# First scans of a hybrid layer: stores of u, delta, gate, B and C on ScalarE's queue, and the product delta times u three turns later

## The chip, the core and the metric

The kernel runs on one core of a Trainium2 chip. Its engines are TensorE (PE, with its weight loads as PEld), VectorE (DVE), ScalarE (ACT), GpSimd (POOL) and SyncE (SP). SP, ScalarE and GpSimd also issue DMAs, each in the order of its own program. The metric is the time of one launch on the device, in microseconds; the median of several launches is given. The profile is of one execution.

## What is computed

Two layers over `x` of shape (4, 64, 64, 128): four images of 4096 tokens with 128 channels. The first layer is a group norm and a state-space block with three scan directions, whose result is added to `x`. The second is an attention layer and a layer of experts. The change lies in the first layer:

```python
xz = einsum('pd,bld->bpl', in_proj_w, x)            # 2 x 256 rows
x, z = split(xz)
x = silu(causal_conv1d(x, conv_w, conv_b))          # u
x_dbl = einsum('rd,bdl->brl', x_proj_w, x)          # 8 rows for delta, 16 for B, 16 for C
delta = softplus(dt_w @ dt_raw + dt_b)
# over l, for each of 256 rows d and 16 states n:
h = h * exp(delta * A) + (delta * u) * B
y = sum_n h * C
out = (y + D * u) * silu(z)                         # z: the gate
```

This is done for three orders of the tokens (forward, backward, sliced), and the three results are added.

## The kernel before

All numbers are float32. A scan of one image and one order is cut into 4 chunks of 1024 tokens. Two kinds of work make it up.

**The inputs** (class `Inputs`). For each image the generator `norm` reads `x`, transposes it, and writes the group norm's result into `xn`. For each of 3 orders and 4 chunks the generator `of_chunk` then does the following. TensorE multiplies `xn` with the input projection, into which the convolution's taps have been folded (L412). ScalarE's Silu writes `u`, two blocks of 128 rows by 1024 tokens (L419). TensorE makes the rows for delta, B and C from `u` (L426), and ScalarE copies them to `xd` (L428). TensorE makes delta's argument (L438), and ScalarE's Softplus writes delta into the tile `r` (L445). For the chunks that `early` names (all twelve of image 0 and the first two of image 1), VectorE multiplies `r` and `u` in place into `u`, as delta times u (L453); for the other chunks that is done later, beside the attention. Everything is stored to DRAM: `keep` (L396) stores `u`, delta and the product in 1 MB each, L439 and L440 store B and C in 64 KB each. The generator `gate` makes silu(z) for a chunk of 1024 tokens and stores it (L379), also 1 MB. All of these stores are issued by SP.

Tiles come from pools: the tag `u` has two buffers, shared by `u` and the gate's `s_g`; `xd` and `r` have one each. A writer of a tile waits until the earlier user of its buffer, a store included, is done.

**The scans** (class `Scans`, generator `of_image`). One step takes 16 rows d by 8 states n, which fill the 128 partitions, over 1024 tokens; image 0 has 384 steps. For each pair of steps `load` brings delta (L527, issued by SP) and delta times u (`du`, L527, issued by ScalarE when the scans of image 0 run alone), each repeated over 8 partitions and so 512 KB; for each four steps a piece of `u` (`us`, L532, SP); and for each chunk B and C (L508, SP). Delta has three buffers, `du` four. ScalarE makes exp(delta * A) (L542). VectorE multiplies du and B into `dB` (L551) and runs the scan into `h` (L561). GpSimd keeps the scan's last column (L563) and multiplies by C (L568). TensorE sums over the states (L599). Every four steps VectorE adds D * u (L615), and SP stores the result `o` (L626, L633 or L637 by the order of the tokens).

**The order.** The program's order on each engine is written out by hand: generators yield, and a loop takes turns between them. Each `yield` of a piece of the inputs is one turn. In the stretch concerned the loop is

```python
first = Pace(decays(nc, dirs, ws, inputs), scans.of_image(0, inputs.made, True))
others = Pace(flow(inputs.pieces(range(nb)), 2, 10))
while not first.done:
    others.run(1.4)
    first.run(1.0)
```

so that 1.4 turns of the inputs of all four images are recorded for each turn of the scans of image 0; a scan step has two turns. `flow` keeps two pieces going and takes a turn of each. The first piece's `decays` loads A in 96 small DMAs on SP (L231). A scan step `s` records the loads of step `s + 4`, the exponential of step `s + 3`, and then its own scan and the dB of step `s + 1`. The scans of images 1 to 3 come later, beside image 0's opening and the attention.

Of the kernel before, what the change touches and what calls it, by code (L numbers as in the profile page):

```python
# [16 lines left out]
P = 128  # L17
# [4 lines left out]
NS = 16  # L22
# [4 lines left out]
T = 1024  # L27
# [3 lines left out]
B_ROW, C_ROW, X_ROWS = 8, 40, 104  # L31
# [180 lines left out]
def orders(b):  # L212

    return ORDERS[min(b, 1)]


def early(b, order, c):

    return b == 0 or (b == 1 and order == orders(b)[0] and c < 2)
# [15 lines left out]
class Inputs:  # L235
# [126 lines left out]
    def gate(self, b, g):  # L362
        nc, xn = self.nc, self.normed[b]
        s_g = self.piece.tile([P, 2, T], F32, tag="u", bufs=2, name=f"z_{b}_{g}")
        banks = yield from self.banks(4, f"z_{b}_{g}")
        for m in range(2):
            for i in range(2):
                at = 3 + g * T + i * 512
                nc.tensor.matmul(
                    banks[2 * m + i], self.w_z[:, m * P : (m + 1) * P], xn[:, at : at + 512], start=True, stop=True,  # L370
                )
            yield
        for m in range(2):
            for i in range(2):
                nc.scalar.activation(s_g[:, m, i * 512 : (i + 1) * 512], banks[2 * m + i], AF.Silu)
                self.leave()
        yield
        yield
        nc.sync.dma_start(out=self.sz[b].rearrange("(m p) t -> p m t", p=P)[:, :, g * T : (g + 1) * T], in_=s_g)  # L379
        self.gated[b] += 1  # L380
        yield

    def of_chunk(self, b, order, c):
        while b not in self.normed or (order == 2 and b not in self.sliced):
            yield WAIT
        src = self.sliced[b] if order == 2 else self.normed[b]
        nc, w, key = self.nc, self.ws[order], f"{b}_{order}_{c}"
        made = {
            "delta": self.dram.tile([DI, T], F32, name=f"d_delta_{key}"),
            "du": self.dram.tile([DI, T], F32, name=f"d_du_{key}"),  # L390
            "u": self.dram.tile([DI, T], F32, name=f"d_u_{key}"),
            "bc": self.dram.tile([2, NS, T], F32, name=f"d_bc_{key}"),
        }

        def keep(name, t):
            nc.sync.dma_start(out=made[name].rearrange("(m p) t -> p m t", p=P), in_=t)  # L396

        def reads(k, g):

            at = c * T + g * 512  # L400
            if order == 1:
                end = L + 6 - at - k
                return src[:, end - 512 : end][:, ::-1]
            return src[:, at + k : at + k + 512]

        halves = [slice(g * 512, (g + 1) * 512) for g in range(T // 512)]
        u = self.piece.tile([P, 2, T], F32, tag="u", bufs=2, name=f"u_{key}")
        banks = yield from self.banks(4, f"cv_{key}")
        for m in range(2):
            for g in range(2):  # L410
                for k in range(4):
                    nc.tensor.matmul(  # L412
                        banks[2 * m + g], w["conv"][:, k, m * P : (m + 1) * P], reads(k, g), start=(k == 0), stop=(k == 3)
                    )
                yield
        yield
        for m in range(2):
            for g, cut in enumerate(halves):
                nc.scalar.activation(u[:, m, cut], banks[2 * m + g], AF.Silu, bias=w["conv_b"][:, m : m + 1])  # L419
                self.leave()  # L420
        yield
        xd = self.piece.tile([X_ROWS, T], F32, tag="xd", name=f"xds_{key}")
        for g, cut in enumerate(halves):
            ps = yield from self.bank(f"xd_{key}_{g}")
            for m in range(2):
                nc.tensor.matmul(ps[:X_ROWS], w["x"][:, m, :], u[:, m, cut], start=(m == 0), stop=(m == 1))  # L426
            yield
            nc.scalar.copy(xd[:, cut], ps[:X_ROWS])  # L428
            self.leave()
        keep("u", u)  # L430
        yield
        r = self.piece.tile([P, 2, T], F32, tag="r", name=f"r_{key}")
        banks = yield from self.banks(4, f"dt_{key}")
        for m in range(2):
            for g, cut in enumerate(halves):
                at = 32 * (2 * m + g)
                rows = slice(at, at + R)
                nc.tensor.matmul(banks[2 * m + g], w["dt"][rows, m, :], xd[rows, cut], start=True, stop=True)  # L438
        nc.sync.dma_start(out=made["bc"][0], in_=xd[B_ROW : B_ROW + NS])  # L439
        nc.sync.dma_start(out=made["bc"][1], in_=xd[C_ROW : C_ROW + NS])  # L440
        yield
        yield
        for m in range(2):
            for g, cut in enumerate(halves):
                nc.scalar.activation(  # L445
                    r[:, m, cut], banks[2 * m + g], AF.Softplus, bias=w["dt_proj_b"][:, m : m + 1]
                )
                self.leave()
        yield
        by_early = early(b, order, c)  # L450
        if by_early:
            for m in range(2):
                nc.vector.tensor_mul(u[:, m, :], r[:, m, :], u[:, m, :])  # L453
                yield
        yield
        keep("delta", r)
        if by_early:
            yield
            keep("du", u)
        self.made[b, order, c] = made  # L460
        yield

# [251 lines left out]
class Attention:  # L714

    def __init__(self, tc, ctx, w, gate, cols, ident, bank, dram, t1, w_out, scans, sz, x):
        nc = self.nc = tc.nc
        gate_w, gate_b = gate  # L720
# [799 lines left out]


def tile_kernel(tc, ctx, x, in_proj_w, dirs, out_proj_w, attn, gate, weight1, weight2, out):


# [13 lines left out]
    with ExitStack() as fill:  # L1538
# [10 lines left out]
        with tc.manual_schedule():  # L1549
# [5 lines left out]
            others.rest()  # L1555
    bank = scans.bank = Bank(ctx.enter_context(tc.tile_pool(name="bank", bufs=1, space=PSUM)), 1)
    block = Attention(tc, ctx, attn, gate, cols, ident, bank, dram, t1, w_out, scans, inputs.sz, x)

    following = Pace(*(scans.of_image(b, inputs.made) for b in range(1, nb)))
# [112 lines left out]
```

## Time and profile before

| | |
|---|---|
| Median of 3 runs | 11419.19 us (11400.92 to 11422.68) |
| The profiled execution | 11412.32 us |
| Its span, first to last instruction | 11410.5 us |
| First dB of image 0's scans starts | 97.97 us |
| Last scan of image 0 starts, and takes | 1800.00 us, 2.35 us |
| Moved by DMA between 60 and 1830 us | 403.68 MB |
| of this on SP's queue (q1), on ScalarE's (q10) | 301.45 MB, 101.11 MB |

The page of a profile gives for each engine the time in which it was busy, and for each group of instructions the idle time ahead of it with the instruction that ended it. An arrow such as "u L453 <- ACT r L445" reads: the instruction that writes `u` in line 453 found its engine idle until ScalarE's instruction of line 445, which writes `r`, was done. "SPq" and "ACTq" are the parts of SP and ScalarE that issue DMAs. The first 1812 us of the span are the stretch in which the scans of image 0 run beside all inputs; after it the opening of image 0 and the attention follow.

The largest DMAs that the inputs and scans of this stretch issue, counted between 60 and 1830 us:

| DMA | by | count | KB each |
|---|---|---|---|
| delta into SBUF, for the scans | SP | 192 | 512 |
| du into SBUF, for the scans | ACT | 192 | 512 |
| u to DRAM | SP | 48 | 1024 |
| delta to DRAM | SP | 48 | 1024 |
| gate to DRAM | SP | 16 | 1024 |
| product to DRAM | SP | 14 | 1024 |
| B and C to DRAM | SP | 96 | 64 |

### The profile page before, as it was taken

How to read it: one execution, taken by the hardware profiler on the slowest of the kernel's cores; microseconds unless marked ns; L12 is line 12 of the kernel's file. 1: busy time of each engine (PE TensorE's matmuls, PEld its weight loads, DVE VectorE, ACT ScalarE, POOL GpSimd, SP SyncE). 2: the span in 40 equal slices, each digit the busy share in tenths (PEclk: the TensorE clock that was granted, in tenths of full speed). 3: DMA queues.
4: the chain of work that ended last, by engine and by line, in shares of the span. 5: the costliest groups of instructions: out<-in, count | busy, mean ns of one | idle time of the engine just before them, and what ended most of it. 6: DMA issues, size and time to landing. Idle time of an engine off the chain costs nothing.

```text
span 11410.5 us, 183033 instructions
## 1 busy us (share of the span) xinstructions
PE 9874.3 (87%) x68358; PEld 3273.6 (29%) x68358; DVE 8258.3 (72%) x8405; ACT 9993.7 (88%) x10828; POOL 3790.3 (33%) x3891
## 2 busy tenths in 40 slices
PE   6687792788998889899998899999998999999995
PEld 2233331222222222222222222222222223333323
DVE  6889997888888987999988979988998321111212
ACT  4566672899999999999999999999999999989992
POOL 4777784332323223424333124243331110000000
PEclk8798895899999999999999999999999999999997
DMA  6778897656565665665656755656556332222225
GB/s 188 226 231 230 226 249 198 161 145 156 142 155 155 178 174 146 158 154 142 151 147 160 194 157 156 156 141 151 146 147 162 116 100 72 76 71 84 75 65 186
DMA packets 900980, 1747.52 MB, mean 153 GB/s; under 512 B 203150, under 2 KB 443846, under 8 KB 899830
## 3 DMA queue, kind: packets, MB, share of 16 engines
q1 hardware_dynamic: 764734, 1469.68, 47.9%
q0 software_dynamic: 93856, 156.41, 4.8%
q10 hardware_dynamic: 41496, 109.71, 3.6%
q8 instruction: 537, 8.80, 0.3%
q14 instruction: 357, 2.92, 0.1%
HBM read 1379.76 MB, written 355.47 MB: 152 GB/s over the span
## 4 chain that ended last, share of the span: by engine, by line
PE 38%; ACT 24%; issue 14%; DVE 11%; DMA 10%; POOL 1%; SPq 1%; ACTq 0%; DVEq 0%; POOLq 0%
PE acc L1012 21%; ACT e L1003 20%; PE s L998 10%; DVE h L561 5%; DMA delta<-d_delta 4%; PE cv L412 2%; DMA du<-d_du 2%; DVE dB L551 1%; ACT dA L542 1%; PE y L599 1%; ACT delta L542 1%; PE fo L1169 1%; PE xd L426 1%; PE h L1156 1%; DMA w<-in_L_ffn_weight_dram 1%
## 5 line engine op out<-in xcount | busy, mean ns | idle before, releaser
L1003 ACT ACTIVATE e<-s 128x1024 f32<-128x1024 f32 x8192 | 7778.1, 1105 | 234.2 <-PE s L998 222.2
L1012 PE MATMUL acc<-e,val 128*32 128x512 f32 x32768 | 5250.2, 615 | 106.5 <-ACT av L1021 93.7
L998 PE MATMUL s<-qm,key 32*128 32x512 f32 x16384 | 2650.8, 501 | 588.8 <-ACT e L1003 558.9
L998 PEld LDWEIGHTS s<-qm,key 32*128 32x128 f32 x16384 | 1013.4, 184 | 4444.4 <-issue 2483.9
L563 POOL COPY ends<-h 128x1 f32<-128x1 f32 x1152 | 1333.8, 1159 | 2362.4 <-DVE h L561 2353.2
L551 DVE TENSOR_TENSOR dB<-du,B 128x1024 f32<-128x1024 f32 x960 | 1213.6, 1264 | 441.2 <-PE y L599 217.2
L1012 PEld LDWEIGHTS acc<-e,val 128*32 128x32 f32 x32768 | 973.5, 109 | 1608.4 <-issue 789.0
L561 DVE TENSOR_TENSOR_SCAN h<-dA,ends,dB 128x1024 f32<-128x1024 f32 x576 | 1351.2, 2346 | 110.3 <-ACT dA L542 66.2
L542 ACT ACTIVATE dA<-delta,A 128x1024 f32<-128x1024 f32 x768 | 935.7, 1218 | 500.5 <-DMA delta<-d_delta 460.8
L561 DVE TENSOR_TENSOR_SCAN h<-delta,ends,du 128x1024 f32<-128x1024 f32 x432 | 1013.2, 2345 | 127.2 <-ACT delta L542 64.3
L568 POOL TENSOR_TENSOR hC<-h,C 128x1024 f32<-128x1024 f32 x384 | 993.5, 2588 | 153.3 <-PE y L599 83.7
L542 ACT ACTIVATE delta<-delta,A 128x1024 f32<-128x1024 f32 x768 | 937.4, 1221 | 7.3 <-DVE dB L551 2.2
L572 DVE TENSOR_TENSOR du<-h,C 128x1024 f32<-128x1024 f32 x576 | 702.2, 1219 | 0.1
L572 DVE TENSOR_TENSOR dB<-h,C 128x1024 f32<-128x1024 f32 x576 | 702.2, 1219 | 0.0
L551 DVE TENSOR_TENSOR du<-du,B 128x1024 f32<-128x1024 f32 x576 | 691.6, 1201 | 5.8 <-DMA B<-d_bc 5.8
L1027 POOL DMA_DIRECT2D d_ctx<-av x512 | 260.3, 518 | 1026.1 <-DVE av L1021 647.6
L412 PE MATMUL cv<-xn,conv 128*128 128x512 f32 x1024 | 469.7, 612 | 26.8 <-DVE xn L346 17.2
L593 POOL DMA_DIRECT2D d_du<-x_delta x272 | 157.2, 578 | 1003.0 <-DVE x_delta L592 945.1
L561 DVE TENSOR_TENSOR_SCAN h<-dA,dB 128x1024 f32<-128x1024 f32 x192 | 438.9, 2286 | 50.3 <-ACT dA L542 40.9
L599 PE MATMUL y<-hC,sel 128*32 128x256 f32 x3072 | 247.8, 456 | 171.7 <-DVE o L615 160.0
L599 PE MATMUL y<-dB,sel 128*32 128x256 f32 x4608 | 378.8, 401 | 9.9 <-DVE xT L1196 4.8
L561 DVE TENSOR_TENSOR_SCAN h<-delta,du 128x1024 f32<-128x1024 f32 x144 | 329.1, 2285 | 68.3 <-issue 35.0
(246 smaller groups left out, 7200.5 us busy)
## 6 DMA issues: line engine op xcount, KB each, us to landing
delta<-d_delta SPq DMA_DIRECT2D x768, 512.0 KB
du<-d_du SPq DMA_DIRECT2D x576, 512.0 KB
du<-d_du ACTq DMA_DIRECT2D x192, 512.0 KB
key<-d_q SPq DMA_DIRECT2D x352, 256.0 KB
d_u<-u SPq DMA_DIRECT2D x48, 1024.0 KB
d_delta<-r SPq DMA_DIRECT2D x48, 1024.0 KB
B<-d_bc SPq DMA_DIRECT2D x96, 512.0 KB
C<-d_bc SPq DMA_DIRECT2D x96, 512.0 KB
```

The source lines that it names most:

```text
L412: nc.tensor.matmul(banks[2 * m + g], w["conv"][:, k, m * P : (m + 1) * P], reads(k, g), start=(k == 0), stop=(k == 3))
L542: nc.scalar.activation(tiles["delta", s], t, AF.Exp, scale=A)
L551: nc.vector.tensor_mul(tiles["du", s], du, spread[order, c, "B", j % 2])
L561: nc.vector.tensor_tensor_scan(h, dA, dB, first, ALU.mult, ALU.add)
L563: nc.gpsimd.tensor_copy(ends[order, c][:, at : at + 1], h[:, T - 1 :])
L568: nc.gpsimd.tensor_mul(tiles["du", s], h, spread[order, c, "C", j % 2])
L572: nc.vector.tensor_mul(dB, h, spread[order, c, "C", j % 2])
L599: nc.tensor.matmul(y[32 * g : 32 * g + 32, : T // 4], self.sel[:, j // 2, :], hC[:, 256 * g : 256 * g + 256], start=(j == 0), stop=(j == 3),)
L998: nc.tensor.matmul(s_ps[:, k, :], keys[f"{i // 4}"][rows, cut].bitcast(F32R), queries[j, qb][rows, :].bitcast(F32R), start=True, stop=True,)
L1003: nc.scalar.activation(e, s_ps, AF.Exp, scale=1.0 / math.sqrt(D))
L1012: nc.tensor.matmul(accs[j, qb][32 * k : 32 * k + 32, :], v[:, k * VW : k * VW + 32], es[i][k // 2][:, k % 2, :], start=(kc == 0), stop=(kc ...
L1027: nc.gpsimd.dma_start(out=self.context[b][h * D : h * D + D, cut], in_=av[32 * k : 32 * k + D, :])
```

## The change

The stores of the gate, of `u`, of delta, and of B and C are issued by ScalarE, directly after the activations or copies that write what is stored, with no turn between. The store of `u` stood behind the copies to `xd`; it now stands ahead of TensorE's work on them. Those of B and C stood behind delta's matmuls; they now stand ahead of them. The product's store stays on SP. The product itself, and its store, are recorded three turns later, except for the first chunk of all. Two turns of the gate and one of a chunk without a product go away.

```diff
@@ gate
                 nc.scalar.activation(s_g[:, m, i * 512 : (i + 1) * 512], banks[2 * m + i], AF.Silu)
                 self.leave()
-        yield
-        yield
-        nc.sync.dma_start(out=self.sz[b].rearrange("(m p) t -> p m t", p=P)[:, :, g * T : (g + 1) * T], in_=s_g)
+        nc.scalar.dma_start(out=self.sz[b].rearrange("(m p) t -> p m t", p=P)[:, :, g * T : (g + 1) * T], in_=s_g)
         self.gated[b] += 1
         yield
@@ of_chunk
         def keep(name, t):
-            nc.sync.dma_start(out=made[name].rearrange("(m p) t -> p m t", p=P), in_=t)
+            nc.scalar.dma_start(out=made[name].rearrange("(m p) t -> p m t", p=P), in_=t)
...
                 nc.scalar.activation(u[:, m, cut], banks[2 * m + g], AF.Silu, bias=w["conv_b"][:, m : m + 1])
                 self.leave()
+        keep("u", u)
         yield
...
             nc.scalar.copy(xd[:, cut], ps[:X_ROWS])
             self.leave()
-        keep("u", u)
+        nc.scalar.dma_start(out=made["bc"][0], in_=xd[B_ROW : B_ROW + NS])
+        nc.scalar.dma_start(out=made["bc"][1], in_=xd[C_ROW : C_ROW + NS])
         yield
...
                 nc.tensor.matmul(banks[2 * m + g], w["dt"][rows, m, :], xd[rows, cut], start=True, stop=True)
-        nc.sync.dma_start(out=made["bc"][0], in_=xd[B_ROW : B_ROW + NS])
-        nc.sync.dma_start(out=made["bc"][1], in_=xd[C_ROW : C_ROW + NS])
         yield
         yield
...
                 self.leave()
+        keep("delta", r)
         yield
         by_early = early(b, order, c)
         if by_early:
+            for _ in range(0 if (b, order, c) == (0, orders(0)[0], 0) else 3):
+                yield
             for m in range(2):
                 nc.vector.tensor_mul(u[:, m, :], r[:, m, :], u[:, m, :])
                 yield
-        yield
-        keep("delta", r)
-        if by_early:
-            yield
-            keep("du", u)
+            yield
+            nc.sync.dma_start(out=made["du"].rearrange("(m p) t -> p m t", p=P), in_=u)
         self.made[b, order, c] = made
         yield
```

## Prediction

> **What bounds the kernel now.** The change lies in the stretch in which the first image's scans run alone beside the making of every scan's inputs. I read the busy time by stretch, then the waits of VectorE, ScalarE and the SP queue there, then the timeline. The stretches (busy us and instructions by engine, granted clock, DMA share, GB/s):
>
> ```profile
> core 0: us, PE busy (x) PEld busy (x) DVE busy (x) ACT busy (x) POOL busy (x), PEclk, DMA share, GB/s
> 60.00:110.00 50.00, 24.70 (x61) 10.00 (x59) 13.27 (x11) 13.73 (x18) 4.79 (x4) 0.77 0.71 175
> 110.00:600.00 490.00, 343.72 (x1424) 137.76 (x1425) 408.29 (x268) 275.57 (x305) 364.07 (x201) 0.80 0.76 224
> 600.00:1200.00 600.00, 488.73 (x2048) 194.42 (x2047) 544.42 (x335) 405.58 (x446) 470.39 (x241) 0.89 0.83 237
> 1200.00:1812.00 612.00, 459.24 (x2072) 184.46 (x2070) 555.01 (x349) 384.79 (x426) 482.94 (x254) 0.86 0.85 225
> ```
>
> VectorE is fullest: 83%, 91%, 91% after the start. Counted by the scan line alone, these three stretches hold 102, 140 and 142 scans: 4.80, 4.29 and 4.31 us each. What a scan needs is read at the end of the stretch, where nothing else runs on VectorE (start, us, instruction):
>
> ```profile
> 1790.89 1.23 DVE L551 TENSOR_TENSOR dB<-du,B 128x1024 f32<-128x1024 f32 x1
> 1792.04 0.64 DVE L615 SCALAR_TENSOR_TENSOR o<-us,D,y 128x256 f32<-128x256 f32 x1
> 1792.53 2.32 DVE L561 TENSOR_TENSOR_SCAN h<-delta,ends,dB 128x1024 f32<-128x1024 f32 x1
> 1794.88 1.23 DVE L551 TENSOR_TENSOR dB<-du,B 128x1024 f32<-128x1024 f32 x1
> 1796.25 2.35 DVE L561 TENSOR_TENSOR_SCAN h<-dA,ends,dB 128x1024 f32<-128x1024 f32 x1
> 1798.63 1.23 DVE L551 TENSOR_TENSOR dB<-du,B 128x1024 f32<-128x1024 f32 x1
> ```
>
> From dB to dB: 3.75 us, 3.99 with the output o, which comes every fourth: mean 3.81. 384 scans take 1463 us; 26 multiplications delta times u (L453) at 1.2 us add 31, the group norms of three images (12 x 1.33, 24 statistics x 0.69, small ones) about 41. That is 1535 of the 1704 us from the first dB (97.97) to the last scan's end (1802.35): 170 us are lost. Where, VectorE's waits say, first of 110 to 600, then of 600 to 1812 (us, times, longest):
>
> ```profile
> DVE u L453 <- ACT r L445: 56.0, 9, 10.5
> DVE stats L319 <- ACT xn L314: 8.7, 1, 8.7
> DVE u L453 <- DMA d_u<-u: 3.4, 1, 3.4
> ```
>
> ```profile
> DVE h L561 <- ACT dA L542: 23.9, 16, 3.6
> DVE dB L551 <- DMA du<-d_du: 20.5, 12, 3.7
> DVE h L561 <- ACT delta L542: 10.6, 11, 2.6
> ```
>
> Early, the product u waits for ScalarE's softplus and the scan stands behind it: 59.4 us. Later it is late exponentials (34.5) and late du (20.5). To these I add dB's own stretch: 384 of them are busy 517.3 us, against 384 x 1.23 = 472; the extra 45 lies in thirty long ones, which I read as du landing late too. So about 100 us late, 60 early. Behind the late exponentials stands SP's queue (its waits, 60 to 1830) and ScalarE's wait for delta:
>
> ```profile
> SPq L527 <- DVE h L561: 240.8, 85, 11.3
> SPq L396 <- ACT u L419: 212.7, 39, 11.6
> SPq L532 <- DVE o L615: 185.0, 50, 7.9
> SPq L439 <- ACT xds L428: 152.2, 43, 8.2
> SPq L396 <- ACT r L445: 69.0, 27, 7.1
> SPq L379 <- ACT z L375: 46.0, 13, 6.4
> ```
>
> ```profile
> ACT dA L542 <- DMA delta<-d_delta: 379.9, 78, 14.2
> ```
>
> 480 us (212.7 + 152.2 + 69.0 + 46.0) of SP's time goes to waiting for ScalarE with delta loads queued behind. From the end of the scan that frees a delta buffer to the issue of the load into it I find 1 to 2 us on average before scan 128, 3 to 7 from there to 358: early SP is not the brake, later it is.
>
> **What the Trainium skill says.** "DMA: Bandwidth & Descriptors", section "Issuing engines are not separate DMA queues": transfers of all issuers share the same 16 engines, and another issuer saves only its sequencer's time. So the 112 stores of 1 MB get no new bandwidth; SP's blocked time is what can be saved. The same page, "Queues, rings and completion order": an engine takes from one ring in order and goes round between rings. The trace has SP's queue at 59.6% and ScalarE's at 21.5% of the engines' time here, which agrees with two rings in use; what a store ahead of a load in ScalarE's ring costs, no run shows yet, since that ring now carries du alone. "Anatomy of one DMA" says a semaphore wait happens on the issuing sequencer before dispatch, and SP's rows above agree.
>
> **The change part by part.**
>
> Start of the scans. SP issues 96 small loads of A until 74.8, and u's store, ready at 66.3, goes out at 74.90; the product waits for it (27.19 us, released by that store) and runs at 79.14, though softplus ended at 73.3. From ScalarE's queue the store leaves at 66.3, so the product runs near 74 and du's store, still on SP, near 76 instead of 81.53. Everything up to the first dB follows: -5 us.
>
> Product three turns later. In the order of the new program the 13 later products stand 2 to 5 scans further on VectorE (6 instead of 4, 14 for 10, 23 for 19), some 10 us or more, as long as the longest wait (10.5). The 59.4 us go. Late next: VectorE then pulls delta and du at the late stretch's pace, and some of that stretch's waits appear here too; 102 scans at the late 1 us loss for every three scans would be 30, of which the freed SP removes half. Net -45 (bounds -59 and -25). The u tile is held longer, two buffers: its next writer stands at least 4 scans after the product in the new order, 15 us against a 1 MB store of some 5; nothing.
>
> Stores off SP. SP loses 208 issues (48 u, 48 delta, 96 B and C, 16 gates) and their 480 us of waits; delta loads go out when their buffer is free, except behind o and us. The 3 to 7 us come off delta, and off du, because du's issue stands on ScalarE behind exponentials that wait for delta. Bound: the whole 100 us.
>
> Their price on ScalarE. An issue took 0.38 us (0.33 for B and C) on SP; on ScalarE each stands behind the activation that it waits for, so it cannot hide beneath it as du's issues do (0.52 us, begun inside an activation). 208 x about 0.45 with the wait is 94 us, beside 672 idle us of ScalarE (1752 - 1080). Hidden on average; an exponential behind it can be 0.5 us later. Table loads rise from 224 to 226 up to the last exponential: 2 x 1.28, hidden.
>
> Their price for du. In the new order 111 of 192 du loads stand directly behind a 1 MB store on ScalarE's queue. At this stretch's 228 GB/s such a store takes 4.6 us, 9 if SP's ring takes half. A du load lands 5.7 us (median) after issue, and is used 17 us after issue before scan 128, about 9 after it. An on-time du would have four scans, 15 us. Early there is room; late, 15 minus activation and issue (about 4) minus 5.7 leaves 5, just a store. I charge 1 us for each of the 79 late ones (bounds 0 and 3). So of the 100 late us, 100 come off if SP was all of it, 80 go back: net -20, bounds -85 and +130.
>
> Fewer turns. The inputs are finished 13 exponentials earlier (last softplus or gate at 354 instead of 367 of 384), so the work is 4% denser; PE is busy 78%, nothing on the path. DMA bytes are the same 404 MB; with 70 us less the mean share rises from 0.81 to 0.85, which the last stretch already holds. Behind 1812 the program's order stays, so what is won here is won at the end.
>
> Sum: -5 - 45 - 20 = -70. The profiled execution took 11412.3 (span 11410.5 and 1.8 around it), 6.9 below the median of 11419.2. 11412.3 - 70 + 6.9 = 11349, say 11350.
>
> **Rivals.** (1) SP was the only brake and the stores hide in the ring's gaps: -5 - 55 - 75 = -135, 11285. For it: 480 us of blocked queue, DMA share only 0.76 early. Against: the last stretch is at 0.85 already. (2) The change moves the blocking without removing it: freed loads wait for their buffers (240.8 us today on h) or for a full DMA, and only the start and part of the product's wait return: -15, 11404. For it: ScalarE's wait for delta stood at 142 us even early, where SP was hardly late. (3) Slower: du behind stores. If each of the 79 late loads costs VectorE 1.7 us more and nothing of the late 100 comes back, +134 - 50 = +84: 11503. It decides from 50 / 79 = 0.6 us each in that case, from 1.9 if the 100 all come back. For it: nine us of lead against 5.7 + 4.6. Against: the lead is that short because ScalarE waits for delta.
>
> **How the numbers follow.** Forecast 0.55 (11310 to 11390), rival 1 0.17, rival 2 0.15, rival 3 0.13. Of this kernel 0.2%, 23 us, can be told from no change. Faster by more (below 11396): 0.55 + 0.17 and a quarter of rival 2, 0.76; within 0.12; slower 0.12. The range, 11275 to 11430, leaves out the upper case and the far end of rival 1.
>
> **What would show it.** Right: no wait of the product for r or d_u; SP waiting for ScalarE near nothing; ScalarE's wait for delta well under 380; first dB near 93; last scan near 1730; 4.4 us a scan early, 4.1 to 4.2 late. Wrong: dB waiting for du beyond 80 us, stretched ones included, or ScalarE's issues grown over 1 us each by a full queue, with exponentials late behind them.

## The result, and the profile after

| | before | after |
|---|---|---|
| Median of the runs | 11418.08 us | 11487.69 us (11471.73 to 11498.88) |
| Ratio of the two, 95% interval | | 1.0063 (1.0045 to 1.0080) |
| Span of the profiled execution | 11410.5 us | 11490.3 us |
| First dB starts | 97.97 us | 106.58 us |
| 128 scans forward, backward, sliced | 604, 558, 539 us | 563, 610, 597 us |
| Last scan of image 0 starts | 1800.00 us | 1878.40 us |

The changed kernel is slower by 0.6%, 70 us by the medians; the prediction was 70 us faster. The fifth row is counted from the scan instructions of the trace, from the first scan of an order to the first of the next (in the third, to its last). It accounts for the 80 us between the spans: 9 lost before the first scan, 41 won in the forward order, 52 lost in the backward and 58 in the sliced one. Behind the last scan nothing differs by more than 2 us.

The busy time by stretch of the changed kernel (the same columns as before the change):

```profile
core 0: us, PE busy (x) PEld busy (x) DVE busy (x) ACT busy (x) POOL busy (x), PEclk, DMA share, GB/s
110.00:600.00 490.00, 350.68 (x1503) 138.23 (x1504) 457.03 (x291) 290.89 (x319) 395.65 (x212) 0.82 0.83 240
600.00:1200.00 600.00, 489.06 (x1985) 195.90 (x1984) 519.90 (x312) 392.38 (x436) 425.61 (x231) 0.88 0.79 226
1200.00:1812.00 612.00, 455.18 (x1896) 182.78 (x1894) 506.71 (x310) 367.75 (x409) 418.05 (x228) 0.84 0.80 213
1812.00:1900.00 88.00, 18.57 (x163) 8.62 (x163) 71.72 (x50) 19.14 (x18) 61.02 (x28) 0.58 0.53 126
```

VectorE gained in the first stretch (457 us busy, 408 before) and lost in the next two (520 for 544, 507 for 555), where the DMA share fell as well, from 0.83 and 0.85 to 0.79 and 0.80. So full DMA engines are not what costs the time. VectorE's waits of 110 to 600, and then of 600 to 1812 (us, times, longest):

```profile
DVE dB L549 <- DMA du<-d_du: 14.8, 9, 3.9
DVE u L454 <- ACT r L443: 3.2, 1, 3.2
```

```profile
DVE dB L549 <- DMA du<-d_du: 75.0, 46, 4.8
DVE h L559 <- ACT delta L540: 56.8, 22, 5.2
DVE h L559 <- ACT dA L540: 14.4, 13, 3.3
```

Early, the product's 59.4 us of waiting are 3.2: the later product does what it was to do. Late, du stands at 75.0 (20.5 before) and the exponentials at 71.2 (34.5 before); of the dB that are stretched beyond 1.4 us there are now 56 with 76 us of excess, 30 with 44 before (what stretches them is read below). SP's queue, 60 to 1830:

```profile
SPq L525 <- DVE h L559: 589.4, 172, 14.2
SPq L530 <- DVE o L613: 548.8, 87, 10.5
SPq L231 <- DMA d_u<-u: 13.9, 1, 13.9
```

SP's 480 us of waiting for ScalarE are gone, and in their place SP waits 1138 us for VectorE, 426 before: its loads stand for a buffer that VectorE has yet to free. ScalarE waits less for delta, too; of the 379.9 us before there are left:

```profile
ACT dA L540 <- DMA delta<-d_delta: 145.0, 29, 13.2
```

So SP was relieved and delta came in time more often, and yet the scans became slower. What ScalarE does meanwhile shows in its timeline around the step that was late at 1275 (start, us, instruction, then idle time and what ended it); ACTq and SPq are the issues of DMAs. After ScalarE stand SP, GpSimd (POOL) and VectorE:

```profile
1260.60 0.33 ACTq L429 DMA_DIRECT2D d_bc<-xds  x1
1260.97 0.43 ACTq L430 DMA_DIRECT2D d_bc<-xds  x1
1261.45 1.15 ACT L540 ACTIVATE dA<-delta,A 128x1024 f32<-128x1024 f32 x1 [0.88 <-DVE dB L549]
1273.32 0.52 ACTq L525 DMA_DIRECT2D du<-d_du  x1
1273.94 1.15 ACT L540 ACTIVATE delta<-delta,A 128x1024 f32<-128x1024 f32 x1 [11.34 <-DMA C<-d_bc]
```

```profile
1264.77 0.53 SPq L530 DMA_DIRECT2D us<-d_u  x1
1265.36 0.54 SPq L506 DMA_DIRECT2D B<-d_bc  x1
1266.00 0.54 SPq L506 DMA_DIRECT2D C<-d_bc  x1
```

```profile
1277.67 2.35 POOL L566 TENSOR_TENSOR hC<-h,C 128x1024 f32<-128x1024 f32 x1 [3.47 <-DVE h L559]
```

```profile
1275.18 2.35 DVE L559 TENSOR_TENSOR_SCAN h<-delta,ends,dB 128x1024 f32<-128x1024 f32 x1 [3.16 <-ACT delta L540]
1277.86 3.25 DVE L549 TENSOR_TENSOR dB<-du,B 128x1024 f32<-128x1024 f32 x1 [0.34 <-DMA du<-d_du]
```

ScalarE does nothing for 11.34 us. It stands at the issue of a du load, and what ends it is the landing of C, with which that load has nothing to do; SP issued C at 1266.00, after its own wait. An exponential and a du are late behind it. VectorE waits 3.16 us for the exponential. For du it waits only 0.34 us, but then the dB takes 3.25 us instead of 1.23. It is not du that stretches it, since du had landed when it started: GpSimd's multiplication hC had begun at 1277.67 and ends at 1280.02, and the dB ends 1.09 us behind it. All 56 stretched dB of this kernel, and all 30 of the kernel before, start while an hC runs and end 1.09 to 1.10 us after it. The other way round, when a dB has begun first, hC takes 3.3 us instead of 2.35. So a dB that misses its place in front of hC can lose up to 2 us more. Of the 56, 40 with 54 us of excess were released by a du; of the 30 before, 10 with 13 us.

The reason is in the program. A completion semaphore is a counter that a DMA raises when it lands. Each DMA that SP or ScalarE issues takes one of eight of them in turn, in the order in which the DMAs are recorded over both queues, and its issuer first waits until the DMA that had this semaphore before, the eighth earlier, has landed. The trace has this: the 1220 DMAs of the two queues up to 1900 us use eight semaphores, this du and C the same one, and ScalarE's wait for it ends at 1273.26, just after C's last count on it at 1273.24. "DMA: Bandwidth & Descriptors" of the Trainium skill, section "Anatomy of one DMA", says that a semaphore wait happens on the issuing sequencer before the dispatch; the 11.34 us agree with that. The page's section "Why a DMA increments its semaphore by 16 and not by 1" gives a reason for waiting at all: where two DMAs in flight share a semaphore, the count can be full before the first has landed. No run here shows that. I call it *standing* where an issue of ScalarE follows within 0.35 us on the landing of the DMA that had its semaphore, and count, up to 1900 us, the time in which nothing else held that issue: 6 us before, 204 after (114 at du's loads, 68 at the stores of B and C, 22 at the rest), nearly all of it for DMAs of SP.

### The profile page after: what moved, and what is told of

Read it like the earlier page. It is cut to its first block, busy times and chain, and to the rows that moved or that the text cites. A ratio compares the mean times of both kernels' runs of the same rounds, so it can differ in the third digit from the quotient of the medians.

```text
span 11490.3 us, 182833 instructions
## 1 busy us (share of the span) xinstructions
PE 9895.7 (86%) x68358; PEld 3280.4 (29%) x68358; DVE 8295.7 (72%) x8405; ACT 9993.1 (87%) x10828; POOL 3760.9 (33%) x3891
## 4 chain that ended last, share of the span: by engine, by line
PE 37%; ACT 23%; issue 14%; DVE 13%; DMA 10%; POOL 1%; SPq 1%; ACTq 1%; DVEq 0%; POOLq 0%
PE acc L1010 20%; ACT e L1001 19%; PE s L996 9%; DVE h L559 6%; DMA delta<-d_delta 3%; DMA du<-d_du 3%; PE cv L410 2%; DVE dB L549 2%; ACT dA L540 1%; ACT delta L540 1%; PE y L597 1%; PE fo L1167 1%; PE h L1154 1%; DMA w<-in_L_ffn_weight_dram 1%; DVE du L570 0%
## 5 line engine op out<-in xcount | busy, mean ns | idle before, releaser
L561 POOL COPY ends<-h 128x1 f32<-128x1 f32 x1152 | 1295.3, 1126 | 2430.0 <-DVE h L559 2402.9
L549 DVE TENSOR_TENSOR dB<-du,B 128x1024 f32<-128x1024 f32 x960 | 1244.8, 1297 | 507.8 <-DMA du<-d_du 269.1
```

The source lines that it names most:

```text
L549: nc.vector.tensor_mul(tiles["du", s], du, spread[order, c, "B", j % 2])
L561: nc.gpsimd.tensor_copy(ends[order, c][:, at : at + 1], h[:, T - 1 :])
```

## The experiments

Each is a short edit, of the kernel after where nothing else is said, and each ratio is to the kernel before. The kernel before ran beside each of them, with a median of 11410 to 11415 us.

**Putting stores back on SP.** There were three theories at first. A: the semaphores that both queues share make ScalarE stand for SP's loads. B: du stands behind a 1 MB store in ScalarE's ring (the prediction's third rival). C: the new places and the turns that went away do the harm. Run 1 puts all stores back on SP (`nc.scalar` to `nc.sync` in lines 377, 394, 429 and 430), at the new places.

> The changed kernel with every store back on SP, at its new place in the order; the product stays three turns later. Theory A (shared completion semaphores: the program hands eight of them round over all DMAs of SP and ScalarE in recorded order, so each DMA waits at its issuer for the eighth DMA before it to land, and ScalarE's stores and du loads now stand still for SP's loads): ScalarE's stalls go, the first 96 steps keep the gain of about 43 us that the changed kernel shows, the late stretch returns to about 139 us per 32 steps, the start to 98: 11370 to 11390. Theory B (du lands late because a 1 MB store lies ahead of it in ScalarE's ring): the same, 11370 to 11390. Theory C (the new order of turns itself does the harm): about 11480.

Measured: 11594.33, 1.0158 (1.0143 to 1.0173). Run 2 puts those of B and C back alone (429, 430), and run 3 the large ones alone (377, 394).

> The changed kernel with only B's and C's stores back on SP; u, delta and gate (all of the 1 MB stores) stay on ScalarE. Theory A: 96 of ScalarE's 400 DMAs and the 68 us that they stood waiting for another DMA's semaphore go: 11430 to 11465. Theory B: B and C are 64 KB, nothing changes: 11475 to 11500.

Measured: 11467.57, 1.0047 (1.0032 to 1.0062): between the two ranges, 3 us above A's and 7 below B's.

> The changed kernel with the 1 MB stores (u, delta, gate) back on SP; only B's and C's stay on ScalarE. Theory A: most of the harm by B and C stays, since they alone stood 68 us at a semaphore and du's loads stand behind them: 11410 to 11450. Theory B: nothing large lies ahead of du any more, so it is as fast as with all on SP: 11370 to 11390.

Measured: 11576.6, 1.0143 (1.0128 to 1.0158). All three theories missed runs 1 and 3. SP's waits of run 1, 60 to 1900, say why:

```profile
SPq L394 <- ACT u L417: 418.2, 47, 21.9
SPq L394 <- ACT r L443: 256.3, 46, 10.6
SPq L429 <- ACT xds L427: 141.1, 44, 7.6
SPq L377 <- ACT z L375: 91.8, 16, 8.9
```

907 us: directly behind the activation, SP waits nearly twice as long for ScalarE as at the old places. So these runs don't undo one thing, they add another, and their totals tell nothing of A. On B, run 3 tells something: without a large store in ScalarE's ring VectorE still waits 55.3 us for du (60 to 1830), against 28.6 in the kernel before.

**One wait taken apart.** In run 4 the load of `us`, for which stores of B and C stood 21 us, is recorded two steps later.

```diff
-            if j == 0:
+            if j == (2 if alone else 0):
...
-                tiles["u", s] = u
+                tiles["u", s - j] = u
```

> The changed kernel with the load of a piece of u recorded two steps later, when its buffer is already free; nothing else. In the changed kernel SP stands 554 us at this load until VectorE's o is done. Theory A: the DMAs of ScalarE that come eight later no longer wait for it (41 us of ScalarE's stalls name it directly, others follow from SP standing there): 11410 to 11460. Theory B: the same bytes in the same rings, no change: 11475 to 11500.

Measured: 11495.08, 1.0075 (1.0058 to 1.0092): no gain. The standing went to the next DMA in the row: du then stood 80 us for SP's delta loads. That goes against A's number, but it does not refute A, since ScalarE stood as long as before, only for another DMA.

**Each part of the change alone.** Run 5: the kernel before, with the product later and nothing else.

```diff
+        late = by_early and not (b, order, c) == (0, orders(0)[0], 0)
+        if late:
+            yield
+            yield
+            yield
+            keep("delta", r)
         if by_early:
             for m in range(2):
                 nc.vector.tensor_mul(u[:, m, :], r[:, m, :], u[:, m, :])
                 yield
         yield
-        keep("delta", r)
+        if not late:
+            keep("delta", r)
...
```

> The kernel before with the product delta times u and its store recorded three turns later, and nothing else; all stores stay on SP, at their old places. Theory C (the new places of the stores and the turns that went away do the harm, the later product is good): VectorE's waits for softplus go, 11365 to 11390. Theory D (the later product itself shifts the input work into the later scans, where it costs more than it saved): 11420 to 11480. Theory E (the harm comes from the issues on ScalarE, wherever they stand): 11365 to 11390, as C.

Measured: 11387.27, 0.9976 (0.9968 to 0.9983): 26 us faster, which goes against D. The orders took 558, 567 and 553 us: 46 won in the forward order, 9 and 14 given back. VectorE's waits of 110 to 600 no longer have the product in a row of weight:

```profile
DVE stats L319 <- ACT xn L314: 7.9, 1, 7.9
DVE xn L346 <- POOL gms L51: 2.6, 1, 2.6
DVE h L569 <- ACT delta L550: 1.3, 1, 1.3
```

Run 6: the kernel before, with the stores issued by ScalarE at their old places (`nc.sync` to `nc.scalar` in lines 379, 396, 439 and 440; the product's store stays on SP).

> The kernel before with the stores of u, delta, gate, B and C issued by ScalarE, but at the old places in the order, the old turns kept and the product not moved. Theory C: ScalarE as issuer is good by itself, SP no longer waits for ScalarE: 11340 to 11400. Theory D: 11380 to 11420. Theory E: ScalarE stands at the issues for semaphores that SP's DMAs hold, late exponentials and late du follow: 11460 to 11540.

Measured: 11500.26, 1.0079 (1.0063 to 1.0096), ScalarE standing 235 us. This part alone costs 87 us, in E's range. Run 7: the changed kernel, with the turns put back behind the stores.

```diff
         nc.scalar.dma_start(out=self.sz[b]..., in_=s_g)
+        yield
+        yield
...
             nc.sync.dma_start(out=made["du"]..., in_=u)
+        else:
+            yield
         self.made[b, order, c] = made
```

> The changed kernel with the turns put back that went away (two of the gate, one of each chunk without a product), now behind the stores. Theory C with the turns as its cause: 11400 to 11440. Theory C with the places as its cause, D and E: no change, 11475 to 11500.

Measured: 11467.7, 1.0050 (1.0035 to 1.0065). The turns that went away cost 20 us, which no theory had: below the loss, but not nothing. By the ratios to the kernel before it is 15 us, about as wide as the intervals. Runs 12 and 14 below, which differ by the same turns, are 32 us apart, so the sign holds. Run 8: both moves at the old places and turns (the edits of runs 5 and 6 together).

> The kernel before with both moves, the stores issued by ScalarE and the product three turns later, but with every other store at its old place and the old turns kept. Theory C: the gains of both add, 11300 to 11360. Theory D: 11430 to 11490. Theory E: 11430 to 11490, the time of the product alone plus what ScalarE's issues cost in the run without the product.

Measured: 11489.88, 1.0069 (1.0054 to 1.0084), standing 306 us. C is refuted by runs 6 and 8: at the old places the loss is as large. E's range holds run 8, at its end. On top of the later product, ScalarE as issuer costs 103 us. Along run 5, run 8, run 7 and the changed kernel the whole adds up to 75 us: -26 for the product, +103 for ScalarE as issuer, -22 for the new places, +20 for the turns.

**Is it the semaphores?** The question is now why the stores cost on ScalarE. Theory A says by standing for semaphores; theory G says by the issues' own time and their wait for the activation ahead. To ease the semaphores without touching ScalarE, runs 9 to 11 store the output `o` of the backward and sliced orders by one DMA instead of four: six DMAs for four steps instead of nine.

```diff
+            if by is nc.sync:
+                n = T // 4 // SLICES
+                if order == 1:
+                    end = L - c * T
+                    to = to[:, end - T : end].rearrange("p (g t) -> g p t", g=4)
+                    by.dma_start(out=to, in_=o)
+                else:
+                    to = to.rearrange("p (i j) -> p i j", i=SLICES)[:, :, 4 * c * n : 4 * (c + 1) * n]
+                    by.dma_start(
+                        out=to.rearrange("p i (g j) -> g p i j", g=4), in_=o.rearrange("p (i j) -> p i j", i=SLICES)
+                    )
+                return
```

> The changed kernel with each output o of the backward and sliced orders of image 0 stored by one DMA instead of four, the bytes and their pieces the same (in the backward order the four quarters of a chunk's result are left unswapped): 192 DMAs fewer on SP, so that the eight completion semaphores that SP and ScalarE share go round more slowly. Theory A (ScalarE stands at its issues for a semaphore that a DMA of SP, eight earlier in the order, still holds): ScalarE's standing of some 204 us falls below 100, 11410 to 11460. Theory G (an issue on ScalarE costs by its own time and its wait for the activation ahead, whatever SP does): 11470 to 11495.

Measured: 11462.41, 1.0042 (1.0025 to 1.0059), 2 us above A's range; standing 147 us instead of 204, and A had said below 100.

> The same single store of o in the kernel with the product three turns later and all stores on SP, the control: SP saves 192 issues of some 0.4 us, and ScalarE hardly stood there (2 us). A and G: 11365 to 11395, against 11387 without it.

Measured, on run 5's kernel: 11440.96, 1.0025 (1.0015 to 1.0035): the control became 54 us slower, which neither theory expected.

> The same single store of o in the kernel whose only change is ScalarE as issuer of the stores at their old places. Theory A: ScalarE's standing falls from 240 us to below 120, 11420 to 11470 against 11500. Theory G: 11480 to 11510.

Measured, on run 6's kernel: 11471.34, 1.0052 (1.0037 to 1.0067), standing 147 us instead of 235: again just above A's range. Since the control moved by itself, the totals decide nothing. The orders tell what they hide (us of the backward and of the sliced order, four DMAs and one):

| kernel | backward | sliced |
|---|---|---|
| run 5, control | 567, 558 | 553, 613 |
| changed kernel | 610, 582 | 597, 600 |
| run 6 | 599, 553 | 573, 584 |

In the sliced order one DMA is costly by itself (+60 in the control). In the backward order it isn't (-9), and there the two kernels with stores on ScalarE gain 28 and 46. That is A's sign, and G has no reason for it. The gain is smaller than A's numbers for the whole, and each order is read from one profiled execution.

**Which queue for du.** Run 12: the changed kernel with du's loads on SP.

```diff
-                by = nc.scalar if alone and name == "du" else nc.sync
+                by = nc.sync
```

> The changed kernel with the du loads of image 0 issued by SP again, so that ScalarE issues stores alone. Theory A: the 114 us that ScalarE stood at du's issues go, 11420 to 11470; more of a loss comes back if SP, blocked at a delta load for a buffer, now holds du up. Theory G: 192 issues of 0.4 us less on ScalarE, 11460 to 11490. Theory B (du behind a 1 MB store in ScalarE's ring): the late du goes, 11400 to 11440.

Measured: 11413.59, 1.0002 (0.9993 to 1.0010): of the loss 4 us are left. That is more than A said, and B's range holds it. But B's mechanism is not what changed: issue to landing of du is 7.2 us (median, from the trace) on SP here, as it is 7.1 behind the stores on ScalarE, and 6.5 before. What changed is when du is issued. With du on ScalarE 71 of 192 loads were issued less than 9 us before their dB (45 in the kernel before); here one is. So as the cause of the late du, B is refuted. A du that is issued while a 1 MB store of ScalarE is under way does land later, on either queue: after 7.7 us in the changed kernel, else after 5.4 (medians), and here, with du on SP, after 8.0 and 6.5.

But SP might be the better queue for du in any case (theory K). So the same edit on run 5's kernel (run 13), on run 7's (run 14), on run 8's (run 16) and on the kernel before (run 17).

> The kernel with the product three turns later and all stores on SP, with the du loads of image 0 on SP too: the control for the run with du on SP and the stores on ScalarE. Theory A (du belongs on the queue that does not stand for the other one's work): SP waits for ScalarE at its stores, and du now stands behind those: 11440 to 11520, against 11387. Theory K (SP is simply the better queue for du, whatever ScalarE stores): 11310 to 11390.

Measured: 11364.9, 0.9956 (0.9942 to 0.9970), in K's range and far from A's.

> The changed kernel with du's loads on SP and the turns put back that went away. The turns gave 20 us in the run where du stood on ScalarE. Theory A, with the turns' effect its own: 11385 to 11405. If the turns helped only by keeping ScalarE's stores apart from du: 11405 to 11420.

Measured: 11381.91, 0.9970 (0.9960 to 0.9980), below both ranges.

> The kernel with both moves at the old places and turns (11490, stores on ScalarE and product later), with du's loads on SP instead of ScalarE. It completes a square: the product later, stores on SP or ScalarE, du on ScalarE or SP: 11387, 11490, 11365 and this. Theory A (the loss comes from du standing among ScalarE's stores; without it ScalarE may store): 11365 to 11395. Theory K (the queue of du and that of the stores cost each by itself and add): 11490 - 22 = 11468, 11455 to 11480.

Measured: 11405.53, 0.9992 (0.9983 to 1.0000), between the two ranges.

> The kernel before with du's loads of image 0 on SP, and nothing else. By the pair with the product later (11387 to 11365) du alone gives 22 us: 11385 to 11400. If it helps only where the product no longer stands in the way: 11405 to 11420.

Measured: 11393.42, 0.9984 (0.9976 to 0.9992), in the first range. The square, with the product later in all four:

| | du on ScalarE | du on SP | du's part |
|---|---|---|---|
| stores on SP | 11387 (run 5) | 11365 (run 13) | -22 |
| stores on ScalarE, same places | 11490 (run 8) | 11406 (run 16) | -84 |
| the stores' part | +103 | +41 | |

Both theories hold in part. SP is the better queue for du by some 21 us, in the kernel before too; 62 us more are an interaction, du's loads among ScalarE's stores; and 41 remain, which stores on ScalarE cost without du. Of these 41, some 9 come ahead of the scans: the first dB starts at 104.0 in run 16 and at 95.4 in run 13. VectorE's waits of 600 to 1812, run 8 and then run 16:

```profile
DVE dB L559 <- DMA du<-d_du: 60.4, 35, 6.9
DVE h L569 <- ACT delta L550: 44.6, 22, 4.9
DVE h L569 <- ACT dA L550: 20.1, 17, 2.2
```

```profile
DVE h L569 <- ACT delta L550: 41.4, 22, 9.6
DVE h L569 <- ACT dA L550: 35.9, 18, 4.3
DVE dB L559 <- DMA du<-d_du: 3.8, 2, 2.5
```

The late du goes, the late exponentials stay: ScalarE still stands 190 us, at its stores. In run 13 it stands for nothing, and the exponentials are all but in time. There du is late instead, behind SP's own waits:

```profile
DVE dB L559 <- DMA du<-d_du: 48.3, 24, 12.5
DVE h L569 <- ACT dA L550: 3.8, 4, 1.6
DVE h L569 <- ACT delta L550: 3.7, 4, 1.2
```

**A version that beats both.** Run 15 takes run 14's kernel, with B and C stored by SP at their old place and the first chunk's product stored by ScalarE ("the run before" in its text is run 14).

> As the run before, and with the B and C stores on SP at their old place behind delta's matmuls, and the first chunk's product stored by ScalarE, so that it does not stand behind SP's loads of A. Theory A: of ScalarE's standing (130 us in the run with du on SP) the 86 at B and C go, and the first dB comes near 97 instead of 106: 11350 to 11385. If SP's waits for xd, with du and delta behind them, take that back: 11390 to 11430.

Measured: 11390.34, 0.9979 (0.9971 to 0.9987). This is the second range. ScalarE's standing fell to 8 us, but the time didn't: SP waits 263.6 us for xd, and now its waits for ScalarE's delta stores come to some 205 us. So the coupling is seen in both directions. So run 18 leaves all stores on SP, as in run 13, and records those of `u`, B and C, the gate, and delta without a product one turn later, with the number of turns the same; SP then finds ScalarE further on.

```diff
-        keep("u", u)
         yield
+        keep("u", u)
...
+        yield
         nc.sync.dma_start(out=made["bc"][0], in_=xd[B_ROW : B_ROW + NS])
         nc.sync.dma_start(out=made["bc"][1], in_=xd[C_ROW : C_ROW + NS])
         yield
-        yield
```

> The kernel with the product later, all stores on SP and du on SP (11365), with every store of u, gate, B and C and of a delta without product one turn later in the order, the number of turns the same. If SP's 388 us of waits for ScalarE still hold up delta and du: half of them go, 11330 to 11355. If the loads then wait for buffers or for each other's semaphores instead: 11360 to 11380.

Measured: 11350.06, 0.9945 (0.9930 to 0.9960): 64 us faster than before, the fastest of all, and in the first range. The orders took 554, 545 and 544 us, against 556, 558 and 548 in run 13. SP's waits for ScalarE, 60 to 1830, are 270 us, 388 in run 13 and 480 in the kernel before; that is a third less than in run 13, where half was expected:

```profile
SPq L396 <- ACT u L419: 126.0, 34, 12.7
SPq L440 <- ACT xds L428: 104.8, 34, 5.7
SPq L380 <- ACT z L375: 22.1, 10, 4.6
SPq L396 <- ACT r L445: 16.6, 12, 4.0
```

## Why the prediction was wrong

**What bounds the kernel** was read rightly in the main: VectorE, held up by the product early and by late exponentials and du later. Two readings were wrong. The 45 us of stretched dB were put down to du; they are hC running ahead of them, and only 13 of the 45 followed on a late du, so the "about 100 us late" held some 30 that du in time could not bring. And ScalarE's wait for delta, 379.9 us, is no measure of loss: it fell to 145.0 in the slower kernel and is 442.9 in run 13, which is faster. That SP's waits for ScalarE cost something agrees with run 18, which has 270 us of them where run 13 has 388, and is 15 us faster; but its stores also stand at other places, and this is not taken apart.

**Start, -5.** Measured +8.6. ScalarE did store `u` early, at 66.80 instead of 74.90. But SP's loads of A then waited 13.9 us for that store (the row L231 above), so that the product's store left SP at 90.17 instead of 81.53. The step followed the store through its queue and left out the semaphore for which SP's next loads had to wait.

**Product three turns later, -45.** Alone -26, at the edge of the bounds. The mechanism was right: of the 59.4 us the forward order got 46. With 30 us for what is late next, and no SP freed, the step's own terms give -29 for run 5; 13 were lost at once and 23 given back in the later orders, 36 in all. So that term was about right; what did not come is the half of it that a freed SP was to take off, since with the stores on ScalarE the later orders lost more, not less (606 and 584 us in run 8).

**Stores off SP, -20.** This is the step that failed: 87 us slower alone (run 6), 103 beside the later product (run 8). Two of its terms were wrong. The price on ScalarE, "Hidden on average", counted 94 us of issue time against 672 idle us; the trace shows 204 us of standing beside it, with du and the next exponential queued behind. And the price for du was put on the ring, 1 us for each late load. By the medians the ring took 0.6 us of landing time (7.1 for 6.5; the prediction had 5.7), and the loads were late because they were issued late. What the step promised of SP did happen, but its loads then stood 712 us more for VectorE. The bounds, -85 and +130, were wide enough for what came, though they don't follow from the step's own terms: with the 100 us won back and 0 or 3 us for each of 79 loads these give -100 and +137.

**Fewer turns, nothing.** Measured +20 (run 7). That the input work is denser was seen, and wrongly called off the path.

**Rivals.** The third gave 11503, 15 us from the result, and that is luck in part: it had the late du right, but put it on the ring, and the loads were late at the issue. The second saw that the freed loads would wait for buffers, and had no reason for a loss. The prediction's first sign of being wrong, dB waiting for du beyond 80 us, came: 97 us, and with the 54 of those that du then left to hC, 151. Its second, issues of ScalarE over 1 us, did not come for the stores (0.94 at most), and for du in 17 of 188 issues (up to 2.58 us; 0.70 at most before); why these took longer is not known.

**What stays open.** That ScalarE stands for SP's DMAs is read in the trace, and that fewer DMAs between them help is shown in the backward order. That the semaphores are all of the 62 and the 41 us is argued: a kernel in which the two queues have semaphores of their own was not tried. Why the turns are worth something was not taken apart, and why a dB and an hC do not run at the same time was not either.

## What to carry to other kernels

A DMA moved to another engine brings along all that its issue must wait for, and where queues share a small set of completion semaphores this includes the other queue's DMAs. Look at what had the DMA's semaphore before it (here the eighth DMA ahead), not only at the sequencer's time. Here an engine whose results the scan needs was a poor place for issues while another queue was often blocked, because that queue's waits became its own. To relieve a blocked queue it was better here to record the stores a turn later on the same queue (15 us won) than to give them to ScalarE (41 or 103 us lost). And a long wait of an engine, as ScalarE's for delta, need not be a loss: the kernel with 145 us of it was slower than the one with 443.

## What was not expected of the hardware

In the sliced order the output goes to DRAM in pieces of 64 bytes. One DMA for all four quarters instead of four, with the same pieces and bytes, made that order 60 us slower in the control (553 to 613 us), and the median from issue to landing of the outputs' stores, backward and forward ones included, rose from 6.1 to 9.4 us (from 5.9 to 13.5 in the sliced order, for DMAs of four times the bytes). The Trainium skill, "DMA: Bandwidth & Descriptors", section "Why a DMA increments its semaphore by 16 and not by 1", says that a DMA is spread over as many engines, up to 16, as divide the outermost dimension of both its sides; with the quarters outermost that is 4. The trace agrees: each engine of a DMA ends it with a packet of 4 bytes, and in the middle of the sliced order SP's queue shows 4486 of these with 124 stores of outputs, and 2624 with 31 (the other DMAs the same). Taking 16 for each of the 124, 122 are left for the 31, 3.9 each. In the backward order, with pieces of 1 KB, the same step saved 9 us all the same, so fewer engines alone are not the whole of it; no run here separates them from the short pieces.
